# Graph layer on one core: the first-level edge sums taken by whole octets instead of by single quads

## The chip, the cores and the metric

The kernel runs on one core of one Trainium2 chip. Its time is device microseconds of one launch; below it is the median of several runs. The profile is of one execution, taken by the hardware profiler. Its engines are TensorE (PE, with its weight loads as PEld), VectorE (DVE), ScalarE (ACT), GpSimd (POOL) and the queue of SyncE (SP) that issues plain DMAs.

## The reference

There are 12,500 nodes of 256 features and 200,000 edges, sorted by destination. All values are float32.

```python
edge_index = jnp.stack([src, dst])
xn = _layernorm(x, axis=-1)
x = x + gnn(xn, edge_index, edge_weight, W_gnn) + mix(xn)     # attention without softmax
x = x + ffn(_layernorm(x, axis=-1))                           # 30 iterations

def gnn(h, edge_index, w, W):
    src, dst = edge_index
    msgs = (h @ W)[src] * w[:, None]
    return relu(segment_sum(msgs, dst, 12500))

def step(h):                                                  # one of the 30
    h = h + 0.01 * tanh(h)
    h = h * sigmoid(h)
    h = _layernorm(h, ln_w, ln_b)
    return h @ W.T + b
```

The attention part needs one product over all nodes of keys and values (64 x 64 per head) before any node can have its result; it then is one 256 x 256 matrix for all nodes ("mix" below).

## The kernel before

**Nodes.** The nodes lie in 98 tiles of 128 rows, and these in 25 groups of four tiles (the last has two). A group goes through the 30 iterations; up to five groups are abreast (`ABREAST`), so that one works on TensorE while the others are on VectorE, ScalarE and GpSimd.

**Edges.** The edges lie in 1563 rows of 128. Each row is gathered with one indirect DMA (`gathers`, line 182, issued from GpSimd's queue) from the normed nodes into one of 16 buffers `xg`; a buffer is free again when the matmul that reads it is done. The sums have two levels. First level: four rows make a *quad*, 391 in all. `sum_quad` (lines 226 to 238) multiplies each row by a 128 x 32 selection `sel`, and the four rows of a quad go to four column strips of the TensorE array, 32 columns each (`tile_position`), into the PSUM tile `pq`. Two quads make an *octet*: the even quad starts the accumulation in `pq` and the odd one ends it. Second level: `copy_quads` (ScalarE, line 245) takes the octet's sums out of `pq`, and `add_quads` (line 259) adds them with a second selection `selq` into a ring of sums `pa`, from which `free_nodes` takes finished nodes. The selections are made on VectorE (`selection`, lines 208, 213 and, once per octet, 221).

**Stages.** (1) Load, norm and transpose the nodes, with the edge lists; up to 128 us of the profile. (2) The key-value loop (lines 793 to 811), 76 passes, one tile each, from 128 to 349 us: `pkv` at line 288, `pacc` at line 314. It carries some quads; a running sum `spent`, in microseconds as the author reckons them, decides in which passes (`quad_at`). (3) A chain of small matrices (lines 822 to 862) with five more quads between them (`another_quad`). (4) From 384 us to the end a row of steps written out by the function `plan` (line 871): it plays the work through with fixed costs (`T_PASS` 4.4, `T_MATRIX` 3.5, `T_QUAD` 1.2, `T_GATHER` 1.25, `T_LAND` 6.0) and gives each step one item, a number of quads, and a number of gathers. An item is "mix" (the attention matrix on a group), "W" (the edge sums of a group times the gnn weight; it can come only when all octets that touch the group are summed) or "pass" (one iteration of a group). A group may start its iterations once its "W" is done; two passes of one group are at least four steps apart (`APART`).

In step k the engines get, in this order: the selections for the quads of this step and the next (line 1025), the copy of a finished octet, the transposes of this step's pass (`pt`, line 996), the matrix of the item of step k-1 (`po`, line 1009), the second-level addition, the gathers, the quads, then the elementwise work of the item of step k-2 (tanh on ScalarE at line 955, line 961 on VectorE, silu at 962, statistics at 968, the power on GpSimd at 974) and the normalisation `z` (line 982) for the next two steps. Each engine works its own queue in order.

Of the kernel before, what the change touches and what calls it, by code (L numbers as in the profile page):

```python
# [30 lines left out]
def gps_layer(  # L31
# [97 lines left out]
    NE = EC + (1 if ER else 0)  # L129
    Q = P // (2 * WIN)  # L130
    NQ = -(-NE // Q)
    O = 2 * Q
# [43 lines left out]
    ed = Edges()  # L176

    def gathers(n):
        while n and ed.gathered < min(NE, ed.summed * Q + ROWS):
            t = ed.gathered  # L180
            ed.xg[t] = gx.tile([P, C], F32, name="xg")
            nc.gpsimd.indirect_dma_start(  # L182
                out=ed.xg[t], out_offset=None, in_=xnd,
                in_offset=bass.IndirectOffsetOnAxis(ap=src_i[:, t : t + 1], axis=0),
            )
            ed.gathered += 1
            n -= 1
# [10 lines left out]
    def selections(n):  # L198
        while n > 0 and ed.selected < NQ:
            selection(ed.selected)  # L200
            ed.selected += 1
            n -= 1

    def selection(q):
        t0, nt = q * Q, min(Q, NE - q * Q)
        h = q % 2
        se = ge.tile([P, Q, WIN], F32, name="se", bufs=1)
        nc.vector.tensor_tensor(
            se[:, :nt, :], rel[:, t0 : t0 + nt, None].to_broadcast([P, nt, WIN]),
            iota_f[:, None, :WIN].to_broadcast([P, nt, WIN]), ALU.is_equal,  # L210
        )
        sel = halves[h][q // 2 % 2]
        nc.vector.tensor_tensor(
            sel[:, :nt, h * WIN : (h + 1) * WIN], se[:, :nt, :], ew[:, t0 : t0 + nt, None].to_broadcast([P, nt, WIN]),
            ALU.mult,
        )
        ed.sel[q] = sel
        if h or q == NQ - 1:
            o = q // 2
            selq = ge.tile([P, WIN2], F32, name="selq", bufs=3)  # L220
            nc.vector.tensor_tensor(selq, relq[:, o : o + 1].to_broadcast([P, WIN2]), iota_f, ALU.is_equal)
            ed.selq[o] = selq
# [3 lines left out]
    def sum_quad():  # L226
        q = ed.summed
        nt = min(Q, NE - q * Q)
        last = q % 2 == 1 or q == NQ - 1
        if q % 2 == 0:  # L230
            ed.pq = p_q.tile([P, KC * C], F32, name="pq")[:, :C]
        sel = ed.sel.pop(q)
        for j in range(nt):
            nc.tensor.matmul(  # L234
                ed.pq[j * 2 * WIN : (j + 1) * 2 * WIN, :], lhsT=sel[:, j, :], rhs=ed.xg.pop(q * Q + j),
                start=(q % 2 == 0), stop=last, tile_position=(0, j * 2 * WIN), skip_group_check=True,
            )
        ed.summed += 1

    def copy_quads():  # L240
        if ed.pq is not None and (ed.summed % 2 == 0 or ed.summed == NQ):
            o = (ed.summed - 1) // 2
            rows = min(Q, NE - o * O) * 2 * WIN
            sq = ge.tile([P, C], F32, name="sq")
            nc.scalar.copy(sq[:rows], ed.pq[:rows])  # L245
            ed.pq = None
            ed.sq[o] = (rows, sq)
# [18 lines left out]
    def free_nodes():  # L266
        while ed.freed < NS and last_of[ed.freed] < ed.added:
            j = ed.freed
            gi = j * SLOT // (G * P)
            if gi not in ed.aT:  # L270
                ed.aT[gi] = ge.tile([P, KC, G * P], F32, name="aT", bufs=3)
            c, d = (j % RING) * SLOT, j * SLOT % (G * P)
            nc.scalar.copy(ed.aT[gi][:, :, d : d + SLOT], pa[:, :, c : c + SLOT])  # L273
            nc.vector.memset(pa[:, :, c : c + SLOT], 0.0)
            ed.freed += 1
# [437 lines left out]
    with ExitStack() as ph:  # L713
# [69 lines left out]
            i: f for i, f in zip(range(kv_done + 6, NT, 4), (ffn_1, ffn_2, ffn_3, ffn_4, ffn_5, ffn_6, wo_1, affine))  # L783
        }

        quad_at, spent, n = {}, 0.0, 0
        for t in range(kv_done, NT + 2):
            quad_at[t] = spent > 7.0 + 5.2 * n
            n += quad_at[t]
            spent += 2.5 + (1.1 if quad_at[t] else 0.0)  # L790
        gathers(ROWS)
        selections(1)
        for t in range(kv_done, NT + 2):
            copy_quads()
            free_nodes()
            kv = None
            if t < NT:
                kv = KeyValue(t)
                kv.squares()
                kv.deviations()  # L800
            if quad_at[t]:
                selections(1)
            if t in rest:
                rest[t]()
            if kv:
                kv.normed()
            kv_product(t - 2)
            add_quads()
            if quad_at[t]:
                sum_quad()  # L810
                gathers(Q)

        def another_quad():
            copy_quads()
# [56 lines left out]
    def plan():  # L871
        T_PASS, T_MATRIX, T_QUAD, T_GATHER, T_LAND, T_POW, T_STATS, T_CHAIN = 4.4, 3.5, 1.2, 1.25, 6.0, 1.3, 4.4, 14.0
        now, pool = 0.0, 4.0
        quads, got, started = ed.summed, ed.gathered, []
        whole, based = [], {}
        active, mixed, steps, k = {}, 0, [], 0
        landed = {t: 0.0 for t in range(got)}
        summed, passes = 0, 0
        pows = {}
        while len(based) < len(groups) or active or len(started) < len(groups):  # L880
            item, nq, cost, start = None, 0, 0.0, None
            octets = NO if quads == NQ else quads // 2
            while summed < len(groups) and octets > last_of[min((summed + 1) * G, NT) * P // SLOT - 1]:
                whole.append(summed)
                summed += 1
            ready = [g for g, (last, it, at) in active.items() if last + APART <= k and at <= now + 1.0]

            wanted = whole and mixed <= whole[0]
            if wanted or (not whole and not ready and mixed < len(groups)):
                item, cost = ("mix", mixed), T_MATRIX  # L890
                mixed += 1
            elif whole:
                item, cost = ("W", whole.pop(0)), T_MATRIX
                based[item[1]] = k
            elif ready:

                lead = 0 if len(started) == len(groups) else 1
                g = min(
                    ready, key=lambda g: (
                        active[g][1] + FFN_ITERS * (g // ABREAST) + lead * (g % ABREAST), active[g][0]  # L900
                    ),
                )
                it = active[g][1]
                passes += 1
                item, cost = ("pass", g, it), T_PASS
                if it == FFN_ITERS - 1:
                    del active[g]
                else:
                    active[g] = (k, it + 1, now + T_CHAIN)
                    pows[k + 2] = pows.get(k + 2, 0) + 1  # L910
            if (
                len(active) < ABREAST and len(started) in based and based[len(started)] + 3 <= k
                and (not started or k >= started[-1] + 4)
            ):
                start = len(started)
                started.append(k)
                active[start] = (k + 3, 0, now + 26.0)
                pows[k + 1] = pows.get(k + 1, 0) + 1
                pows[k + 5] = pows.get(k + 5, 0) + 1

            ng, pool = 0, max(pool, now)
            while got < min(NE, quads * Q + ROWS) and pool < now + (T_STATS - T_GATHER if pows.get(k) else max(cost, 1.0)):
                pool += T_GATHER
                landed[got] = pool + T_LAND
                got += 1
                ng += 1
            if pows.get(k):
                pool = max(pool, now + T_STATS) + T_POW * pows[k]
            ahead = 2 * G * P / STEP * (ABREAST + 0.2 + passes / FFN_ITERS)
            while quads < min(NQ, ahead) and nq < (1 if item else 2):  # L930
                if max(landed.get(t, 1e9) for t in range(quads * Q, min(NE, (quads + 1) * Q))) > now + cost:
                    break
                quads += 1
                nq += 1
                cost += T_QUAD
            steps.append((item, nq, start, ng))
            now += max(cost, 1.0)
            k += 1
        return steps
# [77 lines left out]
    item = lambda k: steps[k][0] if 0 <= k < K and steps[k][0] else (None, None)  # L1017
# [4 lines left out]
    for k in range(K + 3):  # L1022
        nq = quads_of(k)
# [27 lines left out]
        gathers(steps[k][3] if k < K else 0)  # L1051
        for _ in range(nq):
            sum_quad()
            if nq > 1 and ed.summed % 2 == 0:
                copy_quads()

        kind2, g2 = item(k - 2)[:2]
        last = kind2 == "pass" and item(k - 2)[2] == FFN_ITERS - 1
# [116 lines left out]
```

## Time and profile before

| | us |
|---|---|
| median of 3 runs | 4166.28 |
| lowest, highest | 4165.76, 4167.11 |
| the profiled execution, its own time | 4167.84 |
| span of its trace, first to last instruction | 4166.0 |
| PE busy in the span | 4095.5 (98%) |
| DVE, POOL, ACT busy | 3397.5, 2588.0, 2544.1 |
| granted TensorE clock, mean | 0.997 |

| stretch (us from the start) | PE busy | DVE | ACT | POOL |
|---|---|---|---|---|
| 220 to 340 (key-value loop) | 119.76 | 77.39 | 41.59 | 90.75 |
| 340 to 500 (small matrices, first steps) | 144.29 | 88.27 | 40.65 | 123.92 |
| 500 to 1000 | 498.56 | 413.01 | 310.37 | 385.07 |
| 2000 to 3000 | 993.17 | 838.90 | 624.39 | 674.10 |
| 3450 to 4166 (no quads left) | 699.46 | 611.43 | 485.98 | 201.63 |

A float32 matmul appears as two matmuls in the trace, one after the other, so a quad is eight of them and a pass of a full group is eight transposes (one each) and sixteen matmuls. Matmuls overlap in the pipeline: a group's busy time is the union of its spans, while its mean is of one span. How long a group of them really takes is read from the start of its first to the start of what follows.

### The profile page before, as it was taken

Reading aid. Unit: us, or ns where it says so; the run is one execution under the profiler, and the core shown is the slowest. Engines: PE = TensorE matmul, PEld = TensorE weight load, DVE = VectorE, ACT = ScalarE, POOL = GpSimd, SP = SyncE. Lnnn points to the kernel's source line nnn. Section 1 sums busy time; section 2 is a strip of 40 time slices with the busy share of each in tenths; the row PEclk is TensorE's granted clock in tenths of the full one; section 3 lists DMA queues with packets and bytes.
Section 4 is the critical chain, followed back from the end, with each engine's and each line's share of the span. In section 5 each row is a group of like instructions: output and inputs, shape, how many; then the busy total and the mean of one; then the engine's idle time right before and its main releaser. Section 6 shows DMA issues by size and latency. Waiting matters only on the chain.

```text
span 4166.0 us, 67989 instructions
## 1 busy us (share of the span) xinstructions
PE 4095.5 (98%) x24201; PEld 3346.7 (80%) x24201; DVE 3397.5 (82%) x7389; ACT 2544.1 (61%) x3762; POOL 2588.0 (62%) x3186
## 2 busy tenths in 40 slices
PE   8998999999999999999999999999999999999999
PEld 5555788888887888888788888888888888788888
DVE  8664788888888888888888888888888888888887
ACT  7431466666666666666666666656666666677776
POOL 3677777777776666666667667667667652222222
PEclk9999999999999999999999999999999999999999
DMA  8434422222222221112221221122222210000000
GB/s 258 120 106 138 142 80 65 77 75 72 71 83 73 60 63 56 56 56 60 89 65 57 67 63 59 54 75 77 66 64 58 65 44 14 16 1 1 1 1 23
DMA packets 147686, 278.35 MB, mean 67 GB/s; under 512 B 28047, under 2 KB 97197, under 8 KB 147341
## 3 DMA queue, kind: packets, MB, share of 16 engines
q0 software_dynamic: 75024, 204.97, 16.9%
q1 hardware_dynamic: 72173, 68.42, 5.3%
q8 instruction: 197, 3.23, 0.3%
q14 instruction: 148, 1.21, 0.1%
q10 hardware_dynamic: 144, 0.52, 0.0%
HBM read 247.68 MB, written 26.12 MB: 66 GB/s over the span
## 4 chain that ended last, share of the span: by engine, by line
PE 81%; DVE 10%; ACT 2%; issue 1%; POOL 1%; DMA 1%; POOLq 0%; ACTq 0%; DVEq 0%
PE po L1009 55%; PE pt L996 14%; PE pq L234 5%; DVE z L982 3%; PE pkv L288 3%; PE pa L259 3%; DVE st L968 2%; DVE s L961 2%; ACT s L955 2%; DMA xg<-xnd,src_i 1%; PE pacc L314 1%; POOL rs L974 1%; DVE f_st L1131 1%; DVE big L1070 0%; ACT s L962 0%
## 5 line engine op out<-in xcount | busy, mean ns | idle before, releaser
L1009 PE MATMUL po<-w,zT 128*128 128x256 f32 x11760 | 2668.0, 380 | 2.5 <-DVE big L1070 1.9
L1009 PEld LDWEIGHTS po<-w,zT 128*128 128x128 f32 x11760 | 2177.9, 190 | 279.6 <-issue 9.5
L182 POOL DMA_INDIRECT xg<-xnd,src_i x1563 | 1594.1, 1020 | 486.5 <-issue 333.3
L961 DVE SCALAR_TENSOR_TENSOR s<-s,po 128x1024 f32<-128x1024 f32 (+1 forms) x725 | 866.6, 1195 | 399.7 <-ACT s L955 398.6
L982 DVE TENSOR_SCALAR z<-s,st,rs 128x256 f32<-128x256 f32 x2940 | 1051.5, 420 | 77.7 <-POOL rs L974 73.8
L962 ACT ACTIVATE s<-s 128x1024 f32<-128x1024 f32 (+1 forms) x750 | 780.5, 1041 | 381.7 <-DVE s L961 376.0
L968 DVE BATCH_NORM_STATS2 st<-s 128x6 f32<-128x512 f32 x1470 | 937.0, 678 | 85.3 <-ACT s L962 85.3
L955 ACT ACTIVATE s<-po 128x1024 f32<-128x1024 f32 (+1 forms) x725 | 731.0, 1008 | 337.9 <-PE po L1009 337.6
L1003 ACT ACTIVATE zT<-pt 128x512 f32<-128x512 f32 x1470 | 800.6, 601 | 97.2 <-PE pt L996 96.4
L996 PEld LDWEIGHTS pt<-ident,z 128*128 128x128 f32 x5880 | 660.4, 142 | 195.6 <-issue 124.1
L996 PE MATMUL pt<-ident,z 128*128 128x128 f32 x5880 | 793.0, 276 | 20.9 <-DVE z L982 20.3
L974 POOL TENSOR_TENSOR rs<-ve,mhalf 128x4 f32<-128x4 f32 (+1 forms) x750 | 773.1, 1031 | 62.4
L972 POOL TENSOR_SCALAR ve<-st 128x4 f32<-128x4 f32 (+1 forms) x750 | 152.7, 204 | 939.6 <-DVE st L968 909.4
L234 PE MATMUL pq<-xg,sel 128*32 128x256 f32 x3126 | 264.6, 392 | 13.8 <-DMA xg<-xnd,src_i 13.8
L245 ACT COPY sq<-pq 128x256 f32<-128x256 f32 x196 | 72.3, 369 | 302.4 <-PE pq L234 302.3
L288 PE MATMUL pkv<-wkv,big 128*128 128x512 f32 x392 | 196.5, 625 | 7.1 <-DVEq L622 5.0
L259 PE MATMUL pa<-selq,sq 128*128 128x192 f32 (+2 forms) x1168 | 181.5, 291 | 1.0 <-ACT sq L245 1.0
L234 PEld LDWEIGHTS pq<-xg,sel 128*32 128x32 f32 x3126 | 65.4, 108 | 140.7 <-issue 114.5
L259 PEld LDWEIGHTS pa<-selq,sq 128*128 128x128 f32 x1168 | 169.5, 191 | 10.9 <-ACT sq L245 2.0
L273 ACT COPY aT<-pa 128x128 f32<-128x128 f32 x196 | 51.4, 262 | 203.7 <-PE pa L259 202.2
L288 PEld LDWEIGHTS pkv<-wkv,big 128*128 128x128 f32 x392 | 68.7, 195 | 73.7 <-issue 68.1
L295 ACT ACTIVATE sq<-pkv 128x512 f32<-128x512 f32 x98 | 58.2, 593 | 102.5 <-PE pkv L288 102.5
(150 smaller groups left out, 1523.8 us busy)
## 6 DMA issues: line engine op xcount, KB each, us to landing
xg<-xnd,src_i POOLq DMA_INDIRECT x1563
xt<-in_x_dram SPq DMA_DIRECT2D x48, 512.0 KB
xnd<-xt SPq DMA_DIRECT2D x24, 512.0 KB
xt<-accw SPq DMA_DIRECT2D x24, 512.0 KB
out_dram<-big SPq DMA_DIRECT2D x24, 512.0 KB
xg<-in_dst_dram SPq DMA_DIRECT2D x6, 128.0 KB
xg<-in_src_dram SPq DMA_DIRECT2D x6, 128.0 KB
xg<-in_edge_weight_dram SPq DMA_DIRECT2D x6, 128.0 KB
```

What stands on the lines that cost most here:

```text
L182: nc.gpsimd.indirect_dma_start(out=ed.xg[t], out_offset=None, in_=xnd, in_offset=bass.IndirectOffsetOnAxis(ap=src_i[:, t : t + 1], axis=0),)
L234: nc.tensor.matmul(ed.pq[j * 2 * WIN : (j + 1) * 2 * WIN, :], lhsT=sel[:, j, :], rhs=ed.xg.pop(q * Q + j), start=(q % 2 == 0), stop=last, ...
L259: nc.tensor.matmul(pa[:, k, c : c + hi - lo], lhsT=sq[:rows, k * P : (k + 1) * P], rhs=selq[:rows, lo - n0 : hi - n0], start=False, stop=( ...
L955: nc.scalar.activation(flat(s, nt), flat(h, nt), AF.Tanh)
L961: nc.vector.scalar_tensor_tensor(sf, sf, 0.01, flat(h, nt), op0=ALU.mult, op1=ALU.add)
L962: nc.scalar.activation(sf, sf, AF.Silu)
L968: nc.vector.bn_stats(st[:, q, :], s[:, q].rearrange("p c j -> p (c j)"))
L974: nc.gpsimd.tensor_tensor(rs[:, :nt], ve[:, :nt], mhalf[:, :nt], ALU.pow)
L982: nc.vector.tensor_scalar(z[:, j, :], s[:, j // 2, :, j % 2], sv[:, j, 1:2], rs[:, j : j + 1], ALU.subtract, ALU.mult)
L996: nc.tensor.transpose(pt[:, i, k, :], z[:, 2 * q + i, k * P : (k + 1) * P], ident)
L1003: nc.scalar.activation(zT[:, 2 * q : 2 * q + 2], pt, AF.Copy, bias=1.0)
L1009: nc.tensor.matmul(po[:, j // 2, :, j % 2] if paired else po[:, j, :], lhsT=lhsT(j, k), rhs=rhs[:, k, :], start=(k == 0 and (j % 2 == 0 or ...
```

## The change

The unit of the first level becomes the octet. In the key-value loop the octets get their own spacing, two quads follow each other in one pass, and their two selections are made together; the first two are made ahead of the loop. The gathers after them come by eight (`O`) and not by four (`Q`). In `plan` a step gets the quads that are missing to a whole octet, or none, and it gets them only when all of the octet's rows are reckoned to have landed. The copy of an octet between two quads of one step is removed, as no step now goes past an octet. Line 1025 is as it was: it makes the selections for the quads of the next step, which are now two at once or none.

```diff
-        quad_at, spent, n = {}, 0.0, 0
+        octet_at, spent, n = {}, 0.0, 0
         for t in range(kv_done, NT + 2):
-            quad_at[t] = spent > 7.0 + 5.2 * n
-            n += quad_at[t]
-            spent += 2.5 + (1.1 if quad_at[t] else 0.0)
+            octet_at[t] = spent > 12.5 + 10.3 * n
+            n += octet_at[t]
+            spent += 2.3 + (2.2 if octet_at[t] else 0.0)
         gathers(ROWS)
-        selections(1)
+        selections(2)
         for t in range(kv_done, NT + 2):
             copy_quads()
             free_nodes()
...
-            if quad_at[t]:
-                selections(1)
+            if octet_at[t]:
+                selections(2)
             if t in rest:
                 rest[t]()
             if kv:
                 kv.normed()
             kv_product(t - 2)
             add_quads()
-            if quad_at[t]:
+            if octet_at[t]:
                 sum_quad()
-                gathers(Q)
+                sum_quad()
+                gathers(O)
...
             ahead = 2 * G * P / STEP * (ABREAST + 0.2 + passes / FFN_ITERS)
-            while quads < min(NQ, ahead) and nq < (1 if item else 2):
-                if max(landed.get(t, 1e9) for t in range(quads * Q, min(NE, (quads + 1) * Q))) > now + cost:
-                    break
-                quads += 1
-                nq += 1
-                cost += T_QUAD
+            n = min(NQ, (quads // 2 + 1) * 2) - quads
+            if n and quads < ahead and max(
+                landed.get(t, 1e9) for t in range(quads * Q, min(NE, (quads + n) * Q))
+            ) <= now + cost:
+                quads += n
+                nq = n
+                cost += T_QUAD * n
             steps.append((item, nq, start, ng))
...
         gathers(steps[k][3] if k < K else 0)
         for _ in range(nq):
             sum_quad()
-            if nq > 1 and ed.summed % 2 == 0:
-                copy_quads()
```

## The prediction

> **What bounds the kernel now.** I read the page first: who is busy, and which chain ended last.
>
> ```profile
> PE 4095.5 (98%) x24201; PEld 3346.7 (80%) x24201; DVE 3397.5 (82%) x7389; ACT 2544.1 (61%) x3762; POOL 2588.0 (62%) x3186
> PE 81%; DVE 10%; ACT 2%; issue 1%; POOL 1%; DMA 1%; POOLq 0%; ACTq 0%; DVEq 0%
> L1009 PE MATMUL po<-w,zT 128*128 128x256 f32 x11760 | 2668.0, 380 | 2.5 <-DVE big L1070 1.9
> L996 PE MATMUL pt<-ident,z 128*128 128x128 f32 x5880 | 793.0, 276 | 20.9 <-DVE z L982 20.3
> L234 PE MATMUL pq<-xg,sel 128*32 128x256 f32 x3126 | 264.6, 392 | 13.8 <-DMA xg<-xnd,src_i 13.8
> ```
>
> TensorE is busy 98% and makes 81% of the last chain; its long groups are hardly ever kept waiting (2.5, 20.9 and 13.8 us in all). So its time is the sum of what is queued on it, if each piece always takes the same. The timeline of TensorE alone, from a quiet stretch, says that it does:
>
> ```profile
> 606.10 0.64 PE L234 MATMUL pq<-xg,sel 128*32 128x256 f32 x8
> 606.67 1.09 PE L996 MATMUL pt<-ident,z 128*128 128x128 f32 x8
> 607.60 3.62 PE L1009 MATMUL po<-w,zT 128*128 128x256 f32 x16
> 611.05 1.04 PE L996 MATMUL pt<-ident,z 128*128 128x128 f32 x8
> 611.92 3.62 PE L1009 MATMUL po<-w,zT 128*128 128x256 f32 x16
> 615.48 0.64 PE L234 MATMUL pq<-xg,sel 128*32 128x256 f32 x8
> 616.04 1.09 PE L996 MATMUL pt<-ident,z 128*128 128x128 f32 x8
> ```
>
> The reader subtracts starts. The matrix takes 3.45 when transposes follow (607.60 to 611.05) but 3.56 when a quad follows (611.92 to 615.48). A quad takes 0.57 (606.10 to 606.67). Transposes take 0.87 after a matrix (611.05 to 611.92) but 0.93 after a quad (606.67 to 607.60). So a quad that stands alone costs 0.10 + 0.57 + 0.06 = 0.72 us. A step without one is 3.45 + 0.87 = 4.32.
>
> One stretch is different, from the end of the key-value loop to the first steps. Here TensorE waits for gathered rows; the timeline of all engines there, with rows left out:
>
> ```profile
> 351.20 0.95 POOL L182 DMA_INDIRECT xg<-xnd,src_i  x1 [0.30 <-issue]
> 352.45 0.95 POOL L182 DMA_INDIRECT xg<-xnd,src_i  x1 [0.30 <-issue]
> 353.71 0.95 POOL L182 DMA_INDIRECT xg<-xnd,src_i  x1 [0.30 <-PE pq L234]
> 354.96 1.12 POOL L182 DMA_INDIRECT xg<-xnd,src_i  x1 [0.30 <-PE pq L234]
> 356.54 0.62 PE L234 MATMUL pq<-xg,sel 128*32 128x256 f32 x2 [0.64 <-DMA xg<-xnd,src_i]
> 357.92 0.62 PE L234 MATMUL pq<-xg,sel 128*32 128x256 f32 x2 [0.76 <-DMA xg<-xnd,src_i]
> ```
>
> GpSimd issues a gather every 1.25 us, without pause, from 125.0 us on; this is its gather number 183 (from 0) at 354.96, so (354.96 - 125.0) / 183 = 1.257 each. The row it brings is multiplied at 357.92, 2.96 us later. Four rows come each 5.03 us, and from 346 to about 400 us the quads keep to that.
>
> **Part 1: two quads in one block.** The planner of before gives no step two quads: 341 steps have one, 459 none. With 45 quads in the key-value loop and 5 behind it, TensorE has 391 separate blocks of L234. In the changed order there are 197: 194 of two quads, 3 of one. Of the 194, 20 are in the loop (40 quads), 172 in steps, and 2 come together around the small matrices. The matmuls are the same, so what counts is the price of a second quad right behind the first.
>
> No row shows that, but the inside of a quad does. Its eight matmuls are two rounds over the four strips, and take 0.64 us from first start to last end; the shortest single one is 0.379, so the last starts 0.26 after the first, and without the stagger of the four (7 ns each in the trace) a round starts 0.24 after the one before. A second quad is two more rounds on the same strips: 2 x 0.24 = 0.48. Bounds: 0.43, if rounds follow at the 0.216 spacing of the full-size matmuls (3.45 / 16), and 0.72, if it costs what a lone one costs. I take 0.48, as weights already change between the two rounds at that pace.
>
> A rule speaks against this. The Trainium skill, "TensorE: Matmul & The Clock Gate", Part 3, says that a weight load overlaps matmuls in flight only if they use other row groups. All strips here use all rows, so each round would have to wait for the last one and then load: by the trace's 0.109 per load, 0.216 + 0.109 = 0.33 or more, a second quad 0.65, and a pair would save 0.07, 14 us over 194. But the second round's loads start 26 ns after the first round's first matmul, under it, and the 0.24 has no room for the load in series. I go by the row. The 0.15 us around a lone quad agrees with "TensorEngine Tiling (Array Packing)", Key Properties: a change of the tiling mode drains the array; inside a pair there is no change.
>
> Saved per pair: 0.72 - 0.48 = 0.24. In all 194 x 0.24 = 46.6 us (4.8 in the loop, 41.8 later), all on the engine that sets the end. Bounds 0 and 194 x 0.29 = 56.
>
> **Part 2: fewer quads early.** The loop sums 40 quads instead of 45. Before, it ends at 348.8. It loses 20 x 0.24 = 4.8, five quads of 0.71 (3.6, deferred) and two second-level additions of 0.8 (1.6, deferred): end near 338.8. Its own gather waits were about 1 us; eight gathers take 10.06 us and an octet comes about each 9.9, from a start with some 7 us in hand, so it stays about free of them.
> Then the first matrix of the steps. Before, it starts at 384.5, held by rows. Now 46 quads stand ahead of it, 184 rows, the last one number 183, usable at 357.9 as above; quad and matrix follow at 358.5. The small matrices' own chain (four TensorE groups of 1 to 2 us and the copies between them) is shorter than the 19 us from 338.8, and lies under it. So this point comes 26 us earlier: 4.8 are the pairs, 5.2 are deferred work, 16 are waiting that goes away. In the next 15 steps TensorE waited some 6 us before; now the octet in the step of the first matrix wants row 191, usable at 368.0, with the matrix done at 362: about 5. Net 17. Bounds: 8, if octets wait for eight rows twice as long as that, and 23, if the rest goes too.
>
> **Part 3: moved instructions.** *Selections.* Two quads' selections now stand together on VectorE: 2 x (0.205 + 0.225) + 0.358 = 1.22 us, ahead of that step's other work; before it was 0.43 or 0.79. A pass is 3.9 us there (four z 1.43, line 961 1.20, two statistics 1.28), so 5.1 against TensorE's 4.32: 0.8 late. Behind them stand line 961, z and the statistics, for which ScalarE, GpSimd and the transposes wait. But z is made a step or two ahead, and the next step, with the octet, gives TensorE 5.5 against 3.9. Free while that cover holds; without it 0.8 per octet. In the loop VectorE is busy 77 of 120 us and `pkv` has three buffers: free.
> *Gathers.* 1563 as before; a step still issues at most three or four. The step that holds the octet issues for buffers freed an octet earlier, so GpSimd's waits for TensorE to free a buffer (66.6 us in all) should shrink, not grow; the statistics' power behind them on that queue gains. An octet's last gather is at least one step ahead of it in the new order. The old one had 84 quads with one step, and TensorE waited for no row after 440 us.
> *Steps.* 800 before and after, none empty, last quad in step 623 in both. But by the planner's reckoning groups 3 and 4 start 147 and 284 us into the steps instead of 107 and 228, group 9 at 1000 instead of 919, so 158 passes instead of 104 follow the same group's last at only four steps. All of TensorE's waits for z are 20.3 us; laid on those 104, 0.2 each, 54 more are 11. The long stretches at four steps (550 to 640 us) show none; I take 3 of 0 to 11. SP's loads (512 KB each) move with their items, one item a step as before, and lie under whole steps. The removed copy was never reached: nothing.
>
> **Sum.** 4166.0 - 46.6 - 17 + 3 = 4105 for the span. The profiled execution was 1.8 above its span and 1.6 above the median of the runs: 4105 for the median too.
>
> **Rivals.**
> *A, likeliest (0.62):* as summed, 4105. Its own range 4090 to 4122, from 0.48 +/- 0.05 per second quad (10 us) and the waits.
> *B (0.16): the change doesn't do what it says: the second quad costs nearly what the first does* (the load rule, 0.65, to a full drain, 0.72). For: no pair was ever in the trace. Against: the 0.24 between rounds. 4166 - 17 + 3 = 4152, by the load rule 4138.
> *C (0.14): TensorE gets ahead, and VectorE or the chain of a group hands it back.* VectorE is busy 839 of 1000 us in the middle; for it speaks that the selections come in lumps and more groups follow at four steps. With 11 us for these and 0.1 per octet for the lumps (19): 4166 - 64 + 30 = 4132.
> *D, slower (0.08): octets wait for their eighth row.* An octet needs half of the 16 buffers landed at once. If GpSimd is one gather (1.25 us) late for each of the some 100 octets in the steps 20 to 420, where the new plan lags behind its own look-ahead, that is 125: 4166 - 64 + 125 = 4227. It decides from 0.33 us per octet over all 194. Against it: in that stretch 44 to 47 gathers stand in 20 steps, where before up to 54 stood and were met.
>
> **How the numbers follow.** Within 0.2% (8 us) a measurement of this kernel can't tell a difference. A, B and C end faster, 0.92 together, less 0.03 for B or C with costs added to within 8 us: faster 0.89, same 0.03, slower 0.08. The range takes A and C, the low end with 0.43 per second quad and 23 us of waits (4166 - 56 - 23, about 4087), and the high end with B by the load rule: 4085 to 4140.
>
> **What would show it.** Lines L234 of sixteen matmuls, about 1.1 us in the timeline, with the next group 1.05 us after their start; more than 1.2 means B. The first matrix of the steps near 358 us. No row of `pq` waiting for a DMA after 450 us, else D. TensorE's waits for z under 31 us, else C. The stretch without quads at the end stays 4.32 per step and 720 us long; if it grows, I am wrong about where the time is.

## The result and the profile after

The changed kernel takes 4120.28 us (median of 4 runs, 4116.52 to 4122.87) against 4166.69 for the kernel before beside it: a ratio of 0.9888, 95% interval 0.9871 to 0.9905. That is 46 us less, clear of noise, in the range, and three quarters of the 61 that were forecast. The profiled execution took 4122.39, its span 4120.6. From the page of the changed kernel, the lines that answer to those shown of before (the line numbers are up to two higher now):

```profile
PE 4041.8 (98%) x24201; PEld 3376.7 (82%) x24201; DVE 3404.6 (83%) x7389; ACT 2529.2 (61%) x3762; POOL 2576.2 (63%) x3186
PE 80%; DVE 10%; ACT 3%; issue 2%; POOL 1%; DMA 0%; POOLq 0%; ACTq 0%; DVEq 0%
L1011 PE MATMUL po<-w,zT 128*128 128x256 f32 x11760 | 2668.5, 380 | 3.0 <-DVE big L1070 2.1
L998 PE MATMUL pt<-ident,z 128*128 128x128 f32 x5880 | 786.9, 275 | 32.5 <-DVE z L984 31.8
L234 PE MATMUL pq<-xg,sel 128*32 128x256 f32 x3126 | 217.5, 386 | 8.2 <-DMA xg<-xnd,src_i 8.1
```

TensorE still sets the end, with the same counts of instructions. Two columns moved. The quads' busy time fell from 264.6 to 217.5 us, and what ended the idle time before the transposes, the normalised values z from VectorE, grew from 20.3 to 31.8 us.

The timeline of TensorE in a quiet stretch of the changed kernel (start, length, then the group):

```profile
1703.53 1.04 PE L998 MATMUL pt<-ident,z 128*128 128x128 f32 x8
1704.40 3.62 PE L1011 MATMUL po<-w,zT 128*128 128x256 f32 x16
1707.95 1.07 PE L234 MATMUL pq<-xg,sel 128*32 128x256 f32 x16
1708.95 1.09 PE L998 MATMUL pt<-ident,z 128*128 128x128 f32 x8
1709.88 3.62 PE L1011 MATMUL po<-w,zT 128*128 128x256 f32 x16
1713.34 0.81 PE L259 MATMUL pa<-selq,sq 128*128 128x192 f32 x4
```

A pair takes 1.00 us from its start to that of the transposes (1707.95 to 1708.95); a lone quad took 0.57. The second quad costs 0.43, exactly two rounds of 0.216, and the pair saves 0.72 - 0.43 = 0.29 (0.287 by the medians of these starts). Over 194 pairs that is 56 us, more than the kernel gained. So something was given back.

The profiled execution is one of the longer of its kernel, and the granted clock goes with that: the four runs took 4116.52 and 4118.18 us at a mean of 0.998, 4122.39 and 4122.87 at 0.996. In this profile the clock stood at half in some stretches (0.51 from 128 to 135 us, 0.50 from 360.4 to 367.0). A few us between two profiles can therefore be there without any edit.

To find where, each group of TensorE was measured from its start to the next group's start and set against the shortest of its kind; what is over is called waiting here (time at a lower clock is in it too). The table has these waits in us, by stretch; the rows below the second are experiments told of further down:

| kernel | small matrices | first 80 us of steps | from there to the last quad | behind the last quad |
|---|---|---|---|---|
| before | 23.2 | 7.1 | 27.9 | 19.6 |
| changed | 16.5 | 9.3 | 43.7 | 19.8 |
| changed, profiled again | 15.9 | 8.9 | 43.1 | 19.6 |
| changed loop alone | 15.9 | 6.6 | 25.2 | 19.8 |
| changed plan alone | 27.1 | 7.6 | 38.4 | 22.7 |
| pairs split | 20.5 | 4.0 | 35.4 | 19.8 |
| selections spread | 16.6 | 8.1 | 38.8 | 19.6 |
| order of before, 3 gathers a step | 15.9 | 9.0 | 46.5 | 19.5 |

The account of the change: 55.7 gained from pairs; 6.7 less waiting around the small matrices; 2.2 more in the first steps; 15.8 more after them. That is 44.4, against 45.4 between the two spans.

### The profile page after: what moved, and what is told of

The parts are those of the page before. It is cut to its first block, busy times and chain, and to the rows that moved or that the text cites. A ratio compares the mean times of both kernels' runs of the same rounds, so it can differ in the third digit from the quotient of the medians.

```text
span 4120.6 us, 68082 instructions
## 1 busy us (share of the span) xinstructions
PE 4041.8 (98%) x24201; PEld 3376.7 (82%) x24201; DVE 3404.6 (83%) x7389; ACT 2529.2 (61%) x3762; POOL 2576.2 (63%) x3186
## 4 chain that ended last, share of the span: by engine, by line
PE 80%; DVE 10%; ACT 3%; issue 2%; POOL 1%; DMA 0%; POOLq 0%; ACTq 0%; DVEq 0%
PE po L1011 55%; PE pt L998 14%; PE pq L234 4%; PE pkv L288 3%; DVE z L984 3%; PE pa L259 3%; DVE s L963 2%; DVE st L970 2%; ACT s L957 2%; PE pacc L314 1%; POOL rs L976 1%; DVE f_st L1131 1%; DVE big L1070 0%; DMA xg<-xnd,src_i 0%; POOL xg L182 0%
## 5 line engine op out<-in xcount | busy, mean ns | idle before, releaser
L984 DVE TENSOR_SCALAR z<-s,st,rs 128x256 f32<-128x256 f32 x2940 | 1042.8, 419 | 69.4 <-POOL rs L976 67.4
L998 PE MATMUL pt<-ident,z 128*128 128x128 f32 x5880 | 786.9, 275 | 32.5 <-DVE z L984 31.8
L998 PEld LDWEIGHTS pt<-ident,z 128*128 128x128 f32 x5880 | 670.9, 142 | 164.0 <-issue 74.6
L234 PE MATMUL pq<-xg,sel 128*32 128x256 f32 x3126 | 217.5, 386 | 8.2 <-DMA xg<-xnd,src_i 8.1
L234 PEld LDWEIGHTS pq<-xg,sel 128*32 128x32 f32 x3126 | 83.2, 109 | 106.8 <-issue 57.3
```

Source lines behind the costliest of these rows:

```text
L234: nc.tensor.matmul(ed.pq[j * 2 * WIN : (j + 1) * 2 * WIN, :], lhsT=sel[:, j, :], rhs=ed.xg.pop(q * Q + j), start=(q % 2 == 0), stop=last, ...
L984: nc.vector.tensor_scalar(z[:, j, :], s[:, j // 2, :, j % 2], sv[:, j, 1:2], rs[:, j : j + 1], ALU.subtract, ALU.mult)
L998: nc.tensor.transpose(pt[:, i, k, :], z[:, 2 * q + i, k * P : (k + 1) * P], ident)
```

## Experiments

**Are the pairs the gain?** The first quad of each octet goes ahead of the matrix, the second stays behind it:

```diff
         if kind == "pass":
             transposes(gi)
+        if nq == 2:
+            sum_quad()
...
-        for _ in range(nq):
+        for _ in range(1 if nq else 0):
             sum_quad()
```

> The changed kernel, but in each step with an octet its first quad goes ahead of the matrix of the step before and the second stays behind it: same steps, gathers, selections and copies, and 172 blocks of two quads become 344 blocks of one. Theory (a pair saves TensorE one change in and out of the four-strip mode, 0.72 for two lone quads each against 1.00 + 0.15 for a pair, so 0.287 a pair): 172 x 0.287 = 49 us longer than the changed kernel, about 4170 us, a little less if TensorE, now slower, waits less for z. Rival (the gain comes from fewer or later quads around the small matrices, not from the pairs): within 10 us of the changed kernel, 4120 to 4130 us.

Measured: 4169.35 us, ratio to before 1.0009 (1.0000 to 1.0018). The whole gain is gone when the 172 pairs in the steps are split. The timeline of this run shows the lone quads again:

```profile
1702.49 1.04 PE L998 MATMUL pt<-ident,z 128*128 128x128 f32 x8
1703.46 0.64 PE L234 MATMUL pq<-xg,sel 128*32 128x256 f32 x8
1704.03 3.72 PE L1011 MATMUL po<-w,zT 128*128 128x256 f32 x16
1707.68 0.64 PE L234 MATMUL pq<-xg,sel 128*32 128x256 f32 x8
1708.25 1.09 PE L998 MATMUL pt<-ident,z 128*128 128x128 f32 x8
```

The expected 49 us came, though not by its own sum. A quad between transposes and matrix costs a little more than one behind the matrix (transposes 0.97 instead of 0.87 and the matrix 3.65 instead of 3.55, so 0.77 with its own 0.57): 0.05 each, some 8 us over 172. Against that, the waits are 9.6 us fewer in all than in the changed kernel, 8.3 of them between the first steps and the last quad. (Ahead of the first matrix they are 4.0 more: there the first quad of the next octet, whose rows had not come, now stands ahead of the matrix.) The two nearly cancel.

**Which half of the change does what?** One run has the loop of the change with the plan of before, the other the plan of the change with the loop of before. Their diffs are the halves of the one shown.

> The kernel before, with the key-value loop alone as changed (20 octets there, then single quads). Theory: 22 pairs at 0.287 are 6 us, and TensorE waits some 5 us less for gathered rows at the small matrices; about 4155 us. Rival (most of the gain is the waiting for rows that goes away when five quads fewer are in the loop, 17 us as first reckoned): about 4143 us.

> The changed kernel with the key-value loop of before (45 single quads), so that only the steps take octets. Theory: 170 pairs at 0.287 are 49 us, less some 10 to 16 us of new waits for z (137 passes at four steps, between the 104 of before and the 158 of the changed kernel); about 4129 us. If the order makes these waits they are about 0.6 of what the changed kernel has over the one before, if the lumps of selections make them they are all there. Rival (the steps gain nothing by pairs): 4160 us or more.

Measured: loop alone 4145.66 (4145.65 to 4147.2), ratio 0.9952 (0.9935 to 0.9969), 20 us less. Plan alone 4136.26 (4135.2 to 4138.99), ratio 0.9929 (0.9912 to 0.9945), 29 us less. The sum, 49, is the whole change within the noise. The loop gave more than its pairs: 22 pairs are 6.3, and the table shows 7.3 less waiting around the small matrices and 2.7 less later; the rest, some 4 us, is no more than what profiles differ by ahead of the steps. The plan gave less than its pairs: 170 are 48.8, and 10.5 of waits are new after the first steps, 3.9 around the small matrices and 3.1 behind the last quad.

**Where do the new waits come from?** Most of them lie on z. The waits of TensorE over 0.15 us between 440 and 3400 us, before, changed, and with the pairs split:

```profile
PE pt L996 <- DVE z L982: 9.9, 15, 2.0
PE po L1009 <- DVE big L1070: 1.9, 3, 1.3
```

```profile
PE pt L998 <- DVE z L984: 20.7, 25, 2.5
PE po L1011 <- DVE big L1070: 2.1, 2, 1.3
```

```profile
PE pt L998 <- DVE z L984: 18.4, 22, 2.3
PE po L1011 <- DVE big L1072: 0.7, 1, 0.7
```

(In each line: total, times, longest.) One of those of the changed kernel in its timeline, VectorE and TensorE alone:

```profile
541.93 0.20 DVE L208 TENSOR_TENSOR se<-rel,iota_f 128x64 f32<-128x64 f32 x1
542.17 0.23 DVE L213 TENSOR_TENSOR sel<-se,ew 128x64 f32<-128x64 f32 x1
...
542.43 0.23 DVE L208 TENSOR_TENSOR se<-rel,iota_f 128x64 f32<-128x64 f32 x1
...
542.69 0.22 DVE L213 TENSOR_TENSOR sel<-se,ew 128x64 f32<-128x64 f32 x1
542.83 0.35 DVE L221 TENSOR_TENSOR selq<-relq,iota_f 128x192 f32<-128x192 f32 x1
543.10 1.21 DVE L963 SCALAR_TENSOR_TENSOR s<-s,po 128x1024 f32<-128x1024 f32 x1
544.23 2.68 DVE L984 TENSOR_SCALAR z<-s,st,rs 128x256 f32<-128x256 f32 x8
...
544.78 1.32 PE L998 MATMUL pt<-ident,z 128*128 128x128 f32 x8 [1.21 <-DVE z L984]
```

The two quads' selections, a lump of 1.2 us, stand on VectorE ahead of z, and the transposes wait 1.21. This looked like the cause. The test makes the first of the two selections one step earlier:

```diff
-        selections(ed.summed + nq + quads_of(k + 1) - ed.selected)
+        selections(ed.summed + nq + quads_of(k + 1) + quads_of(k + 2) // 2 - ed.selected)
```

> The changed kernel, but the selection of an octet's first quad is made two steps ahead of it and that of the second one step ahead, so VectorE has 0.43 and 0.79 us of them in two steps and not 1.22 in one. Theory (the waits of the transposes for z that are new in the changed kernel, 20.7 us against 9.9 between 440 and 3400 us, come from two selections in a lump ahead of z on VectorE): these waits fall to about 12 us and the time by 5 to 15 us, to about 4110 us. Rival (they come from the order: 158 passes instead of 104 follow the same group's last at only four steps): waits and time stay, 4117 to 4123 us.

Measured: 4113.56 (4111.37 to 4117.65), ratio 0.9878 (0.9862 to 0.9895). The ratio's interval overlaps that of the changed kernel, so the gain is not certain. In the profiles part of it lies ahead of the steps: the loop ended 4.6 us earlier in this one, with the same code up to there, and the clock from 128 to 150 us was 0.98 instead of 0.84. Between runs of the same mean clock some 5 us are left (at 0.998, 4111.44 against 4116.52 and 4118.18; at 0.996, 4117.65 against 4122.39 and 4122.87). The waits for z in that window fell only from 20.7 to 18.5, all waits to the last quad from 43.7 to 38.8. So the lump is worth some 5 us of the 16, as far as one profile each can tell.

The rival was the order of the steps. To have pairs and lumps in the order of single quads, the steps were planned as before, and then each even quad was held back to its odd one (the lines of `plan` that are as before are left out):

```diff
...
+        quads, got, held, owed, whole_octets = ed.summed, ed.gathered, 0, 0, []
+        for item, nq, start, ng in steps:
+            held, owed = held + nq, owed + ng
+            n = (NQ if quads + held == NQ else (quads + held) // 2 * 2) - quads
+            g = min(owed, min(NE, quads * Q + ROWS) - got)
+            whole_octets.append((item, n, start, g))
+            quads, got, held, owed = quads + n, got + g, held - n, owed - g
+        return whole_octets
```

> The changed kernel, but the steps are planned as before (quads one at a time, from the 45 that the key-value loop and the small matrices leave), and only then each even quad is held back to the step of its odd one. So the items, their order and the starts of groups are those of the run with the changed loop and single quads (114 passes at four steps, not 158), while pairs and lumps of selections are those of the changed kernel. Theory (the order makes the new waits): 172 pairs at 0.287 below that run's 4145.7, so 4096 to 4099 us, with 25 to 28 us of waits between 440 and 3400 us. Rival (lumps of selections, or TensorE being faster, make them): waits of 35 us or more, 4105 to 4112 us.

Measured: 4515.35 (4508.22 to 4521.18), on a chip where the kernel before took 4239.06; ratio 1.0651 (1.0633 to 1.0669). Neither theory had that. What it did is in GpSimd's timeline of this run:

```profile
2003.00 1.07 POOL L182 DMA_INDIRECT xg<-xnd,src_i  x1 [0.17 <-issue]
...
2010.70 0.96 POOL L182 DMA_INDIRECT xg<-xnd,src_i  x1 [0.30 <-issue]
2011.73 0.20 POOL L980 TENSOR_SCALAR ve<-st 128x4 f32<-128x4 f32 x1
2012.01 1.03 POOL L982 TENSOR_TENSOR rs<-ve,mhalf 128x4 f32<-128x4 f32 x1
```

Seven gathers stand in one step, 8.7 us, and the power of the statistics waits behind them. VectorE's z then waits for it; the line of all waits in this run:

```profile
DVE z L990 <- POOL rs L982: 431.2, 301, 5.7
```

In the changed kernel that wait is 67.4. Held quads had freed eight buffers at once, and 78 steps issued seven gathers. Not all of the loss is waiting: against the run of the first octet on the same chip (told below; span 4199.5), TensorE was idle for 182 us more and busy for 130 us more with the same instructions (4203.4 against 4073.6), while the mean granted clock was 0.966 and not 0.990. The mend allows three in a step (`g = min(..., 3)`), and was run beside the changed kernel and two more on one chip:

> The changed kernel as it is, beside the next three on one chip: 46 us below the kernel before.

> The run with the steps planned as before and even quads held back, but with at most three gathers in a step; without that bound 78 steps had seven gathers ahead of the statistics' power on GpSimd's queue, which is what is now held to have cost it 350 us. If so, that goes away whole. Then, against the changed kernel beside it: theory (the order, 158 passes at four steps against 114, makes the new waits for z) 10 to 20 us faster, with 25 to 30 us of waits between the first steps and the last quad. Rival (lumps of selections, or TensorE being faster, make them): within 6 us of the changed kernel, with 38 us or more of waits. If it is still 100 us slower, the gathers were not the cause.

Measured: the changed kernel again 4118.76 (4117.88 to 4120.98), ratio 0.9888; the order of before with three gathers 4123.32 (4119.5 to 4127.1), ratio 0.9900 (0.9883 to 0.9916). The loss was the gathers, and it went whole. And with 114 passes at four steps and not 158, the waits are 46.5 us to the last quad, not fewer. The wait of z for the power, which the gathers delay, is 104.0 here and 67.4 in the changed kernel, so this run has a load of its own and does not prove that the order does nothing; it shows that the order alone does not bring the waits down.

**The pause of the gathers.** In the changed kernel the 17th gather (number 16) leaves 2.2 us late (3.4 us behind the 16th, where 1.25 is the pace), as no buffer is free before the first octet. The first octet was put two passes earlier:

```diff
-            octet_at[t] = spent > 12.5 + 10.3 * n
+            octet_at[t] = spent > (12.5 + 10.3 * n if n else 7.5)
```

> The changed kernel, but the first octet of the key-value loop stands two passes earlier (7.5 instead of 12.5 in the loop's reckoning), the other 19 as they were. In the changed kernel each gather from number 159 on leaves 4.0 us later than before. Theory (with 16 buffers taken, GpSimd pauses until the first octet frees eight): the pause goes, gather 183 leaves near 355 us instead of 359, the first matrix of the steps comes 3 to 5 us earlier, and the time falls by 3 to 5 us. Rival (the delay comes later, or the rows are held up by the loads of the first steps alone): no change beyond 2 us.

> The changed kernel with only the first octet two passes earlier, beside the changed kernel on one chip. Theory: GpSimd's pause after the 16th gather (2.5 us in the changed kernel) goes and the first matrix of the steps and the end come 2 to 4 us earlier. Rival: no change beyond 2 us, as the rows are held by the loads of the first steps.

The first of these two ran on the chip where before took 4239.06: 4204.94, ratio 0.9922 (0.9906 to 0.9939). There the loop itself was some 50 us longer, so it says nothing on a pause of about 2 us. The second: 4120.04 (4119.28 to 4120.61), against 4118.76 beside it. No gain. Gather 16 leaves 1.2 us after number 15 (2.4 in the run beside it), so the pause there is gone, but gathers 24 to 48 take 31.5 us instead of 30.2, and gather 183 leaves at 356.2 instead of 356.8. The second octet stands where it did and frees its buffers no earlier, so the pause moved one octet on.

**Put together.** Three runs combined the parts:

> The order planned as before with even quads held back, the selections spread over two steps, and the first octet two passes earlier, together. If the three add up: 4097 less 2 to 4 for the selections and 4 for the first octet, about 4090 us. If they hit the same waits: not under 4097.

> As the run with all three, but of the five quads between the small matrices only the first two stay and three more go to the steps. Theory (TensorE waits there for rows that come at 1.25 us each, while the first steps have matrices that need none): the first matrix of the steps comes 8 to 12 us earlier and about 5 to 8 us of it stay, about 4083 us. Rival (the small matrices' own chain is as long as the rows' wait): the time stays, since the waits are TensorE's waits for that chain.

> The run before this in the list, with the selections spread over two steps and the first octet two passes earlier: 5 to 8 us below it if these add up, 3 for the selections and 4 for the first octet.

The first two had the seven gathers and the slow chip: 4460.14 and 4452.09 (ratios 1.0522 and 1.0504). Beside each other they differ by 8 us, and the first matrix of the steps came at 408.0 instead of 412.0; this would fit quads being better placed in the steps than between the small matrices, but their intervals overlap, so it is not shown. The third, with three gathers at most, took 4116.07 (4115.19 to 4118.18), ratio 0.9880 (0.9863 to 0.9896), 2.7 below the changed kernel beside it and 7.3 below the run it adds to. By these intervals no version is clearly faster than the changed kernel.

## Why the prediction was right, and where it was off

*What bounds the kernel:* right. TensorE's groups kept their lengths to 0.01 us, and the stretch without quads is 720 us as before (from 3400.3 to the end).

*Part 1, pairs:* the mechanism is right and the split shows it. The second quad was put at 0.48; it is 0.43, the low bound. The 0.24 between the first two rounds stands in a pair too, but the third and fourth follow at 0.216, so the 0.024 was a price of the first round, not of every round. The term is 55.7, not 46.6. The rule by which the prediction weighed B (the Trainium skill, "TensorE: Matmul & The Clock Gate", Part 3) does not hold for these column strips: with its load in series the second quad would have taken 0.65, and it took 0.43.

*Part 2, fewer quads early:* right in sign, too large: 17 forecast, 6.7 less waiting at the small matrices and 2.2 more in the first steps, so 4.5. The first matrix came at 364.1, not 358.5, and took 5.01 us instead of 3.56, as the granted clock stood at 0.50 there. Two things were left out: the stream of gathers runs 4.0 us later (1.4 in its start, which varies by run, and most of the rest in the pause), and the rows for the last quad came later than 2.96 us after their issue. The wait in the timeline of the changed kernel:

```profile
355.11 0.40 SPq L89 DMA_DIRECT2D xt<-in_x_dram  x1
355.20 0.95 POOL L182 DMA_INDIRECT xg<-xnd,src_i  x1 [0.30 <-PE pa L259]
...
355.74 0.41 SPq L1038 DMA_DIRECT2D xt<-accw  x1
...
361.08 1.06 PE L234 MATMUL pq<-xg,sel 128*32 128x256 f32 x2 [3.70 <-DMA xg<-xnd,src_i]
```

The gather issued at 355.20 is multiplied at 361.08, 5.9 us later, and two loads of 512 KB had been issued on SP's queue beside it. That these loads delayed it is only argued; no run moved them. If they did, "SP's loads ... lie under whole steps" was right of time on TensorE and overlooked what they do to the rows.

*Part 3, moved instructions:* this is the step that failed. "I take 3 of 0 to 11" for new waits became 15.8, outside its bounds. The selections were called free while z is made a step or two ahead; that cover fails near the start of a group: of the waits for z between 440 and 3400 us, all but two begin within 26 us behind a group's first normalisation (line 1131). The kernel before has its waits at the same places, fewer of them. Spreading the selections took off 4.9. With the pairs split (same order, same lumps, TensorE slower) the waits are 35.4, which is 7.5 above before and 8.3 below the changed kernel; by the waits for z alone, 8.5 of the 10.8 new us stay. So half or more comes from what was moved, and the rest only when TensorE runs ahead. The bound of 11 was laid on the passes at four steps; fewer of these, 114, went with no less waiting. What makes the rest is open; no run separates VectorE's load from the gathers' place on GpSimd's. As forecast, GpSimd's waits for quads to free a buffer shrank, from 66.6 to 23.0.

*Rivals:* B (the pair saves nothing) is out by the split. C is partly true: its sign, waits for z of 31 us or more, was just met (31.8), and the way it named is the way the time went back, half its size. D didn't occur: TensorE waited for no row after 400 us.

The sum is 15 us off, because an error of 9 in one direction made up for part of two of 12 to 13 in the other. That is luck: with the pairs at 46.6 the time would have been near 4130, outside the range of A itself (4090 to 4122), in which 4120.28 just lies.

## What to carry to other kernels

On an engine that is never kept waiting, measure groups from start to start with and without the neighbour in question: the price of an interruption (here 0.29 us of 0.72) can be read that way, and grouping interruptions is worth their number times that price. Then ask how near the next engine is to full, since each step that gets shorter takes cover from it; here 15.8 of some 62 us went there. Work that is moved should keep its pace on shared queues: eight buffers freed together let seven gathers go ahead of one small operation that every pass needs, and that run took 6.5% longer than the kernel before.

## What the runs showed of the hardware

A change from full-size matmuls into four column strips cost 0.10 us, and one out of them 0.06 when transposes followed and 0.10 when a matrix followed (run with the pairs split). Rounds on the same strips started 0.240 us apart at first and 0.216 from then on, the full-size pace. In a lone quad the loads of the second round start 27 ns after the matmuls of the first, on the same rows.

Gathers left GpSimd's queue every 1.25 us where nothing held them, and the queue kept the program's order: in the run with seven in a step, the power stood behind 8.7 us of them.

The kernel before took 4166 us beside most runs and 4239 in one batch, on another chip. There the key-value loop was slower: in the run with only the first octet moved, its passes from the 29th to the 97th `pkv` took 238.1 us, against 189.4 for the same kernel in the other batch. The mean granted clock was 0.990 and 0.997. What was lacking there was not found, and whether the chip makes it is open, as no other batch ran on it.
